# State space stage: decay factors of four of eight steps in three SBUF tiles, products with B up to four steps ahead, preparation dealt out by a table

## The chip, the cores and the metric

The kernel runs on one core of a Trainium2 chip. The core has engines that run side by side, each with its own queue of instructions in a fixed order: PE (TensorE, matrix products and transposes), DVE (VectorE), ACT (ScalarE), POOL (GpSimd) and SP (SyncE, which here issues all DMA transfers). Data lie in SBUF, a memory of 128 partitions that all engines reach, and in PSUM, eight small banks per partition, into which PE writes and which DVE and ACT can read and write. POOL works on SBUF alone in this kernel.

The metric is the time of one execution on the device in microseconds (us). Before the change it is 4334.76 us, the median of three runs (4333.15 to 4337.2). The profiled execution is one more run, with its own time.

## The reference

The model is a chain of six residual blocks over an input of 16 sequences (batches) of 512 positions with 256 channels, all float32: a feed-forward block with fp4 quantisation, a state space block (the block of this change), the feed-forward block again, a mixture of low-rank experts, attention with a distance bias, and the experts again. The state space block, cut to its core:

```python
xz = hidden_states @ W_in                      # 256 -> 2 * 512
x, z = jnp.split(xz, 2, axis=-1)
x = silu(causal_depthwise_conv(x, conv_w, 4 taps) + conv_b)
proj = x @ W_x                                 # dt_low (16), B (16), C (16)
dt = softplus(dt_low @ W_dt + b_dt)
A = -exp(A_log)                                # 512 channels x 16 states
def step(h, (dt_t, x_t, B_t, C_t)):
    h = exp(dt_t[..., None] * A) * h + (dt_t * x_t)[..., None] * B_t[:, None, :]
    return h, einsum('bds,bs->bd', h, C_t)
y = (scan over the 512 positions) + x * D
return (y * silu(z)) @ W_out
```

For each channel and each of 16 states this is a linear recurrence over 512 positions: h = a * h + b, with a the *decay factor* exp(dt * A) and b the *product with B*, dt * x * B. The result is multiplied with C and summed over the states.

## The kernel before

**Tiling.** `mamba_phase` (L469) walks through 16 batches `b`. A batch has four groups `c` of 128 channels and, in each group, eight *steps* `k`, so 32 steps per batch (`s`) and 512 in all (`t`). A step handles 128 channels and two of the 16 states per channel group: partitions hold four state groups of 32 channels each, and the free dimension holds two rows of 512 positions, 1024 elements. `k // 2` is the quarter `q` of the states, `k % 2` the half of the channels.

**One step.** ACT writes the decay factors with two activations (`factors`, L940: exp with a per-partition scale). POOL writes the product with B (`make_bx`, L863, tile `bx`). DVE runs the recurrence as one `tensor_tensor_scan` of 1024 elements (L971), whose inputs are the factors and the product. Column 0 of each row of the factors is zero, so that the second row starts afresh. The result is multiplied with C into a tile `g`: on DVE (L486) when the scan wrote to PSUM (tile `h`), on POOL (L483) when it wrote to SBUF (tile `hs`, two buffers); the flag `other` tells which. Before the change, POOL takes the product with C in steps 0, 2, 3 and, in even groups, 6. PE adds up the states: `accumulate` (L900) multiplies a pair of `g` tiles with a folding matrix into one PSUM bank `y`. After a group's last pair, `finish_mult` (L809) multiplies `y` into `zs` on DVE, right after the scan of step 0 of the next group.

**Where the inputs of the scan lie.** Two PSUM tiles `das` (two banks each) hold decay factors of the even and odd steps. In steps 4 and 5 (`turned`, quarter `TQ` = 2) it is the other way round: PE writes the product with B into the `das` tile with 32 small matmuls (`turn_bx`, L886; its second operand `diag` is made on POOL by `diagonals`, L874), and ACT writes the factors into one of two SBUF tiles `sides` (named `ds0` and `ds1`; the tile that holds dt, loaded from DRAM, is named `ds` too). So each of the eight scans has one input in PSUM and one in SBUF. After a turned scan DVE clears column 0 of its `das` tile again (L977).

**Order.** The order on every engine is the order in which the program issues (`keep_in_program_order`). In step `t` it issues: the product with B for step t + 2, the factors for step t + 1, the scan, `accumulate` for a pair that is due, the DMA issues of the step, one or two pieces of the preparation, `turn_bx` for step t + 2, and the product with C.

**Preparation.** `prepare` (L624) is a generator that computes all inputs of the next batch (transposes, input projection, the four convolution taps as four matmuls per channel group, W_x, softplus, dt * x, and the output projection of an earlier batch through `out_half`). Between its pieces it yields; 36 pieces per batch are dealt out, one per step, and two in steps 24, 26, 28 and 30. Most pieces are PE work that goes through a single PSUM bank (`mm`), followed by an ACT copy.

**Transfers.** SP issues all DMAs: `fetch_steps` (L553) loads dt and dt * x of the next channel group, spread over partitions, in two times four transfers, dealt out by the table `PIECES`; `fetch` (L541) loads a row pair of B and C, broadcast over partitions (tile `bc`); `later` writes dt and dt * x to DRAM.

Of the kernel before, what the change touches and what calls it, by code (L numbers as in the profile page):

```python
# [9 lines left out]
F32 = mybir.dt.float32  # L10
# [6 lines left out]
P = 128  # L17
NB, SEQ, D = 16, 512, 256
# [19 lines left out]
def macaron_kernel(  # L38
# [430 lines left out]
    def mamba_phase(w, src, dst):  # L469
        with tc.tile_pool(name="m1", bufs=1) as m1, tc.tile_pool(  # L470
# [17 lines left out]
            def pe(out, **kw):  # L488
                tc.keep_in_program_order(nc.tensor.matmul(out, **kw))  # L489
# [17 lines left out]
                nc.vector.memset(da[:, :, 0:1], 0.0)  # L507
                das.append(da)
            sides = []
            for i in range(2):  # L510
                da = m1.tile([P, 2, SEQ], F32, name=f"ds{i}")
                nc.gpsimd.memset(da[:, :, 0:1], 0.0)  # L512
                sides.append(da)
# [110 lines left out]
            def prepare(b):  # L624
# [15 lines left out]
                def taps(c):  # L640

                    if b == 0:
                        return
                    q = mm()
                    for k in range(DCONV):
                        pe(
                            q, lhsT=cwd[:, DCONV * c + k, :], rhs=xps[c % 2][:, k : k + SEQ],
                            start=(k == 0), stop=(k == DCONV - 1),
                        )
                    return q  # L650
# [47 lines left out]
                    to_xp(c, p)  # L698
                yield from project_out(0)
                for c in range(2):  # L700
                    p = taps(c)
                    yield
                    to_u(c, p)
                    p = in_proj(xT, c + 2)
                    yield
                    to_xp(c + 2, p)
                yield from project_out(1)
                for c in range(2, NDC):
                    p = taps(c)
                    yield  # L710
                    to_u(c, p)
                p = mm()
# [96 lines left out]
            def finish_mult(b, c, y):  # L809
                zs = zss[b]  # L810
                vec(zs[:, c, :], zs[:, c, :], y, ALU.mult)
# [27 lines left out]
            def close():  # L839

                for half in range(2):
                    for _ in range(6):
                        yield
                    for _ in out_half(NB - 2, half):
                        yield

            def where(t):
                return t // STEPS, t // NP % NDC, t % NP

            PIECES = (  # L850
# [4 lines left out]
            )  # L855
            bxs, ys, done = {}, [], []

            def run_later():
# [40 lines left out]

            def accumulate(b, c, q, gs):  # L900
                if q == 0:
                    ys.append(ps_y.tile([P, SEQ], F32, name="y", tag="y"))
                    u = state[b][0][c // 2][:, c % 2, :]
                    for i in range(0, P, 32):
                        pe(
                            ys[0][i : i + 32, :], lhsT=dskd[i : i + 32, c, :],
                            rhs=u[i : i + 32, :], start=True, stop=False,
                        )
                for i in range(4):
                    pe(  # L910
                        ys[0][32 * i : 32 * i + 32, :], lhsT=fold,
                        rhs=gs[i // 2][:, i % 2, :], start=False, stop=(q == NQ - 1),
                    )
                if q == NQ - 1:
                    done.append((b, c, ys.pop()))

            def flat(t):
                return t.rearrange("p n s -> p (n s)")
# [12 lines left out]
            for q in range(NQ):  # L931
                fetch(0, q)
            spare.clear()
            for t in range(2):
                make_bx(t)
            for _ in diagonals(0):
                pass
            for _ in range(4):
                next(rest)
            def factors(t):  # L940

                b, c, k = where(t)
                if b < NB:
                    q, p = k // 2, k % 2
                    da = (sides if q == TQ else das)[t % 2]
                    for j in range(2):
                        g = 4 * c + 2 * p + j
                        act(
                            da[:, j, 1:], spread[b, c, p][:, j, 0, 1:],
                            AF.Exp, scale=a_neg[:, g, q : q + 1],  # L950
                        )
# [3 lines left out]
            for t in range(STEPS * NB):  # L955
                b, c, k = where(t)
                s = t % STEPS
                if s == 0:
                    ahead = prepare(b + 1) if b + 1 < NB else close()
                    stat = stats(b + 2) if b + 2 <= NB else iter(())  # L960
                make_bx(t + 2)
                factors(t + 1)

                other = k in (0, 2, 3) or k == 6 and c % 2 == 0
                if other:
                    h = m2.tile([P, 2, SEQ], F32, name="hs", tag="hs", bufs=2)
                else:
                    h = ps_h.tile([P, 2, SEQ], F32, name="h", tag="h")
                turned = k // 2 == TQ
                da, bx = (sides, das) if turned else (das, bxs)  # L970
                tc.keep_in_program_order(nc.vector.tensor_tensor_scan(  # L971
                    flat(h), flat(da[t % 2]), flat(bx[t % 2] if turned else bx.pop(t)),
                    0.0, op0=ALU.mult, op1=ALU.add,
                ))
                if turned:
                    tc.keep_in_program_order(
                        nc.vector.memset(das[t % 2][:, :, 0:1], 0.0)  # L977
                    )

                if t in due:  # L980
                    accumulate(*due.pop(t))
                if s == 2:
                    load_out(b - 1)
                if s == 17:
                    load(b + 2)
                if 20 <= s < 24:
                    next(stat, None)

                if k == (0, 0, 0, 2)[c]:
                    steps = fetch_steps(*divmod(b * NDC + c + 1, NDC))  # L990
                for _ in range(PIECES[c][k]):
                    next(steps, None)
                run_later()
                if b and s == 0:
                    fetch(b, NQ - 1)
                if c == NDC - 1 and k in (2, 4, 6):
                    fetch(b + 1, k // 2 - 1)
                for _ in range(2 if t < 8 or s in (24, 26, 28, 30) else 1):
                    next(rest if t < 4 else ahead, None)
                turn_bx(t + 2)  # L1000
                g = m2.tile([P, 2, SEQ], F32, name="g", tag="g", bufs=5)
                C = rows[b, k // 2][:, 1:, :].to_broadcast([P, 2, SEQ])
                if other:
                    pool(g, h, C, ALU.mult)
                else:
                    vec(g, h, C, ALU.mult)
                if s == STEPS - 2:
                    diags = diagonals(b + 1)
                if t >= STEPS - 2 and s in (STEPS - 2, STEPS - 1, 0, 1):
                    next(diags, None)  # L1010
                pair.append(g)
                if k % 2:
                    due[t + 1 + other] = (b, c, k // 2, pair)
                    pair = []
                if k == 0 and done:
                    finish_mult(*done.pop())
                if s == STEPS - 1:
                    for _ in ahead:
                        pass
# [831 lines left out]
```

## Time and profile before

| what | value |
|---|---|
| median of three runs | 4334.76 us |
| time of the profiled execution | 4331.12 us |
| its span, first to last instruction | 4329.4 us |
| first scan of the stage starts at | 626.8 us |
| last scan of the stage starts at | 2503.6 us |
| 610 to 2506 us: PE busy | 1526.4 us of 1896 (80.5%), granted clock 0.90 |
| 610 to 2506 us: DVE busy | 1564.7 us (82.5%) |
| 610 to 2506 us: POOL busy | 1567.7 us (82.7%) |
| 610 to 2506 us: ACT busy | 1276.5 us (67.3%) |

The profiled execution took 1.7 us more than its span, and it lies 3.6 us under the median. Busy time is the time in which an engine has at least one instruction in work; the idle time that a row names is that of the engine just before the row's instructions, with the work that ended it. "Issue" stands where the engine waited for nothing that the profile shows. All the work of this change lies in the stage between about 610 and 2506 us; the other blocks are not touched.

### The profile page before, as it was taken

How to read it: one execution, taken by the hardware profiler on the slowest of the kernel's cores; microseconds unless marked ns; L12 is line 12 of the kernel's file. 1: busy time of each engine (PE TensorE's matmuls, PEld its weight loads, DVE VectorE, ACT ScalarE, POOL GpSimd, SP SyncE). 2: the span in 40 equal slices, each digit the busy share in tenths (PEclk: the TensorE clock that was granted, in tenths of full speed). 3: DMA queues.
4: the chain of work that ended last, by engine and by line, in shares of the span. 5: the costliest groups of instructions: out<-in, count | busy, mean ns of one | idle time of the engine just before them, and what ended most of it. 6: DMA issues, size and time to landing. Idle time of an engine off the chain costs nothing.

```text
span 4329.4 us, 68272 instructions
## 1 busy us (share of the span) xinstructions
PE 3833.4 (89%) x26498; PEld 2127.4 (49%) x26498; DVE 3629.7 (84%) x5002; ACT 2310.5 (53%) x3543; POOL 1844.9 (43%) x1687
## 2 busy tenths in 40 slices
PE   7999967888888888887888689999999999999989
PEld 4666632333333333333333356666765555555547
DVE  9999848888888888888888889998877888888876
ACT  4444337666666676677666534443534444444444
POOL 1000028888888888888888800000301111111121
PEclk9999988998999999999999889999999999999999
DMA  4000035444455545545444420000000000000002
GB/s 141 15 15 20 15 93 123 118 117 110 109 133 126 131 110 133 132 114 128 121 117 110 104 108 1 1 1 1 13 20 18 15 19 18 21 16 19 19 13 69
DMA packets 120471, 292.63 MB, mean 68 GB/s; under 512 B 30721, under 2 KB 50754, under 8 KB 120146
## 3 DMA queue, kind: packets, MB, share of 16 engines
q1 hardware_dynamic: 120146, 288.26, 26.2%
q8 instruction: 208, 3.41, 0.3%
q14 instruction: 117, 0.96, 0.1%
HBM read 209.26 MB, written 62.13 MB: 63 GB/s over the span
## 4 chain that ended last, share of the span: by engine, by line
PE 64%; DVE 13%; POOL 9%; ACT 7%; issue 3%; DMA 3%; SPq 1%; DVEq 0%; ACTq 0%; POOLq 0%
PE s L1180 10%; PE p L489 8%; PE g L289 7%; PE u L289 7%; PE o L325 7%; PE p L1180 4%; PE y L489 4%; POOL bx L483 4%; PE o L489 3%; PE p L1183 3%; POOL g L483 3%; DVE h L971 3%; PE da L489 3%; PE o L1180 3%; DMA ds<-dd 2%
## 5 line engine op out<-in xcount | busy, mean ns | idle before, releaser
L483 POOL TENSOR_TENSOR bx<-ds,bc 128x1024 f32<-128x1024 f32 x384 | 900.8, 2364 | 106.4 <-DVE h L971 91.7
L483 POOL TENSOR_TENSOR g<-hs,bc 128x1024 f32<-128x1024 f32 x224 | 526.9, 2365 | 201.6 <-DVE hs L971 196.7
L480 ACT ACTIVATE da<-ds,a_neg 128x511 f32<-128x511 f32 x768 | 526.7, 688 | 147.5 <-DVE da L977 73.0
L1351 ACT ACTIVATE eT<-s 128x768 f32<-128x768 f32 (+1 forms) x384 | 338.7, 882 | 420.3 <-PE s L1180 420.3
L1357 POOL TENSOR_SCALAR_AFFINE_SELECT eT<-eT 128x256 f32<-128x256 f32 (+1 forms) x384 | 189.9, 495 | 863.4 <-ACT eT L1351 863.4
L971 DVE TENSOR_TENSOR_SCAN hs<-da,bx 128x1024 f32<-128x1024 f32 x224 | 505.2, 2276 | 37.1 <-POOL bx L483 33.5
L489 PE MATMUL y<-g,fold 128*32 128x512 f32 x2048 | 380.0, 679 | 134.2 <-DVE g L486 101.7
L1180 PE MATMUL s<-k,q 32*128 32x256 f32 (+3 forms) x2048 | 459.6, 470 | 9.1 <-DVE mx L1311 5.8
L971 DVE TENSOR_TENSOR_SCAN h<-ds,da 128x1024 f32<-128x1024 f32 x128 | 293.8, 2296 | 171.9 <-issue 72.9
L971 DVE TENSOR_TENSOR_SCAN h<-da,bx 128x1024 f32<-128x1024 f32 x160 | 366.8, 2292 | 75.7 <-issue 27.4
L1311 DVE TENSOR_REDUCE mx<-s 128x2 f32<-128x1024 f32 (+3 forms) x512 | 410.1, 822 | 12.5
L1180 PE MATMUL s<-qm,k 32*128 32x512 f32 (+3 forms) x2048 | 385.7, 471 | 17.9 <-ACT eT L1351 11.4
L486 DVE TENSOR_TENSOR g<-h,bc 128x1024 f32<-128x1024 f32 x288 | 350.7, 1218 | 13.0
L1307 DVE TENSOR_TENSOR s<-s,mask 128x256 f32<-128x256 f32 (+1 forms) x384 | 198.8, 518 | 154.6 <-PE s L1180 144.4
L489 PE MATMUL p<-xT,w_in 128*128 128x512 f32 x500 | 271.6, 670 | 57.4 <-ACT dT L480 33.4
L294 ACT ACTIVATE sl<-g 128x352 f32<-128x352 f32 x256 | 118.3, 464 | 381.4 <-PE g L289 370.4
L1180 PEld LDWEIGHTS s<-k,q 32*128 32x128 f32 x2048 | 206.3, 185 | 171.1 <-issue 93.6
L1508 POOL TENSOR_TENSOR g<-rs,v 128x4 f32<-128x4 f32 x64 | 13.2, 211 | 635.7 <-ACT rs L1505 551.3
L489 PEld LDWEIGHTS da<-diag,dT 128*32 128x32 f32 x8192 | 220.8, 111 | 69.7 <-issue 42.0
L489 PE MATMUL da<-diag,dT 128*32 128x128 f32 x8192 | 250.4, 277 | 4.1 <-DVE hs L971 3.1
L489 PEld LDWEIGHTS y<-g,fold 128*32 128x32 f32 x2048 | 55.9, 113 | 368.3 <-DVE g L486 181.4
L512 POOL MEMSET ds<- 128x2 f32 x2 | 0.1, 102 | 531.5 <-DMA xd<-x 531.5
(286 smaller groups left out, 7957.7 us busy)
## 6 DMA issues: line engine op xcount, KB each, us to landing
ds<-dd SPq DMA_DIRECT2D x512, 256.0 KB, 5.2
bc<-bd SPq DMA_DIRECT2D x256, 128.0 KB, 5.6
dd<-dt SPq DMA_DIRECT2D x32, 1024.0 KB, 5.1
x<-_attn_hidden_states_dram SPq DMA_DIRECT2D x16, 512.0 KB, 6.6
xd<-x SPq DMA_DIRECT2D x16, 512.0 KB, 2.6
xo<-xd SPq DMA_DIRECT2D x16, 512.0 KB, 3.6
xe<-xo SPq DMA_DIRECT2D x16, 512.0 KB, 2.8
x<-xe SPq DMA_DIRECT2D x16, 512.0 KB, 10.7
```

What stands on the lines that cost most here:

```text
L289: nc.tensor.matmul(dst, lhsT=xT[:, k, c * P : (c + 1) * P], rhs=w[:, k, f0 : f0 + HF], start=(k == 0), stop=(k == KD - 1),)
L325: last = nc.tensor.matmul(o, lhsT=hT[:, f, :], rhs=wdT[:, f, :], start=(f == 0), stop=False)
L480: return tc.keep_in_program_order(nc.scalar.activation(out, in_, func, **kw))
L483: tc.keep_in_program_order(nc.gpsimd.tensor_tensor(out, in0, in1, op=op))
L486: tc.keep_in_program_order(nc.vector.tensor_tensor(out, in0, in1, op=op))
L489: tc.keep_in_program_order(nc.tensor.matmul(out, **kw))
L971: tc.keep_in_program_order(nc.vector.tensor_tensor_scan(flat(h), flat(da[t % 2]), flat(bx[t % 2] if turned else bx.pop(t)), 0.0, op0=ALU.m ...
L1180: tc.keep_in_program_order(nc.tensor.matmul(out, **kw))
L1307: nc.vector.tensor_tensor(own, own, const["mask"][:, :w].unsqueeze(1).to_broadcast([P, 2, w]), op=ALU.add)
L1311: nc.vector.tensor_reduce(mx[:, t, 2 * pair : 2 * pair + 2, RM], s[:, :, off : off + (t + 1) * P], axis=AX.X, op=ALU.max,)
L1351: const["exp"] = nc.scalar.activation(eT[:, 2 * pair : 2 * pair + 2, e0 : e0 + w], s[:, :, :w], AF.Exp)
L1357: nc.gpsimd.affine_select(out=own, in_=own, compare_op=ALU.is_ge, fill=0.0, base=0, pattern=[[0, 2], [0, n], [1, P]] if n > 1 else [[0, 2] ...
```

## The change

- A third SBUF tile for decay factors. The factors of steps 2, 3, 4 and 5 go to the three `sides` tiles in turn (`factors_at`); the `das` tiles hold the factors of steps 0, 1, 6 and 7 and the turned products of steps 4 and 5. The scans of steps 2 and 3 thereby read both inputs from SBUF.
- The table `FACTORS` says in which step factors are issued, and for how many steps ahead: one step ahead for steps 6, 7, 0 and 1, and two steps ahead for steps 2 to 5, behind the preparation of the issuing step.
- The table `PRODUCTS` does the same for the product with B: three or four steps ahead, behind the product with C of the issuing step. `bx` keeps three buffers.
- `turn_bx` for step 4 is issued in step 2, that for step 5 in step 4, in both cases ahead of the step's preparation.
- POOL takes the product with C in steps 0, 1, 3 and, in even groups, 5. `g` has four buffers where it had five.
- The table `PREPARED` says how many pieces of the preparation are done by each step of the batch (40, since `taps` now yields after two of its four matmul groups), at most three in a step.
- `diagonals` for the next batch is issued in steps 29 (two pieces), 30 and 31, where it was 30, 31, 0 and 1. `PIECES` gives group 1 its last four transfers in steps 1 and 2, where it had steps 3 and 4. `finish_mult` is issued ahead of the product with C of step 0, which is on POOL.

```diff
-            for i in range(2):
+            for i in range(3):
                 da = m1.tile([P, 2, SEQ], F32, name=f"ds{i}")
...
                     for k in range(DCONV):
+                        if k == 2:
+                            yield
                         pe(
...
-            PIECES = (
-                (4, 4, 0, 0, 0, 0, 0, 0),
-                (4, 0, 0, 2, 2, 0, 0, 0),
-                (4, 2, 2, 0, 0, 0, 0, 0),
-                (0, 0, 4, 4, 0, 0, 0, 0),
-            )
+            PIECES = ((4, 4, 0, 0), (4, 2, 2, 0), (4, 2, 2, 0), (0, 0, 4, 4))
+            PREPARED = (
+                (2, 4, 4, 4, 4, 5, 7, 8), (9, 11, 11, 12, 12, 13, 14, 15),
+                (16, 18, 18, 19, 21, 23, 25, 27), (30, 32, 33, 34, 35, 37, 39, 40),
+            )
+            FACTORS = ((1, 2), (2,), (2,), (2,), (), (1,), (1,), (1,))
+            PRODUCTS = ((3,), (), (4,), (4,), (4,), (), (3,), (3,))
...
-            for t in range(2):
+            for t in range(3):
                 make_bx(t)
...
+            def factors_at(t):
+                n, k = divmod(t, NP)
+                return sides[(4 * n + k - 2) % 3] if 2 <= k <= 5 else das[k % 2]
+
             def factors(t):
...
-                    da = (sides if q == TQ else das)[t % 2]
+                    da = factors_at(t)
...
-                make_bx(t + 2)
-                factors(t + 1)
-
-                other = k in (0, 2, 3) or k == 6 and c % 2 == 0
+                if k not in (1, 2, 3):
+                    for n in FACTORS[k][:1]:
+                        factors(t + n)
+
+                other = k in (0, 1, 3) or k == 5 and c % 2 == 0
...
-                da, bx = (sides, das) if turned else (das, bxs)
                 tc.keep_in_program_order(nc.vector.tensor_tensor_scan(
-                    flat(h), flat(da[t % 2]), flat(bx[t % 2] if turned else bx.pop(t)),
+                    flat(h), flat(factors_at(t)), flat(das[k % 2] if turned else bxs.pop(t)),
                     0.0, op0=ALU.mult, op1=ALU.add,
                 ))
...
                 if t in due:
                     accumulate(*due.pop(t))
+                if k == 2:
+                    turn_bx(t + 2)
+                if k == 4:
+                    turn_bx(t + 1)
...
-                for _ in range(2 if t < 8 or s in (24, 26, 28, 30) else 1):
-                    next(rest if t < 4 else ahead, None)
-                turn_bx(t + 2)
-                g = m2.tile([P, 2, SEQ], F32, name="g", tag="g", bufs=5)
+                if t < 4:
+                    for _ in range(2):
+                        next(rest, None)
+                else:
+                    for _ in range(min(3, PREPARED[c][k] - prepared)):
+                        next(ahead, None)
+                        prepared += 1
+                for n in FACTORS[k][k in (0, 4, 5, 6, 7):]:
+                    factors(t + n)
+                g = m2.tile([P, 2, SEQ], F32, name="g", tag="g", bufs=4)
                 C = rows[b, k // 2][:, 1:, :].to_broadcast([P, 2, SEQ])
+                if k == 0 and done:
+                    finish_mult(*done.pop())
                 if other:
                     pool(g, h, C, ALU.mult)
                 else:
                     vec(g, h, C, ALU.mult)
-                if s == STEPS - 2:
+                for n in PRODUCTS[k]:
+                    make_bx(t + n)
+                if s == STEPS - 3:
                     diags = diagonals(b + 1)
-                if t >= STEPS - 2 and s in (STEPS - 2, STEPS - 1, 0, 1):
+                    next(diags, None)
+                if s >= STEPS - 3:
                     next(diags, None)
...
-                if k == 0 and done:
-                    finish_mult(*done.pop())
```

More of the change, by code (lines that the diff above doesn't have):

```diff
@@ L700, in prepare @@
                 for c in range(2):
-                    p = taps(c)
+                    p = yield from taps(c)
                     yield
@@ L708, in prepare @@
                 for c in range(2, NDC):
-                    p = taps(c)
+                    p = yield from taps(c)
                     yield
@@ L958, in mamba_phase @@
                 if s == 0:
+                    prepared = 0
                     ahead = prepare(b + 1) if b + 1 < NB else close()
                     stat = stats(b + 2) if b + 2 <= NB else iter(())
-                make_bx(t + 2)
-                factors(t + 1)
-                other = k in (0, 2, 3) or k == 6 and c % 2 == 0
+                if k not in (1, 2, 3):
+                    for n in FACTORS[k][:1]:
+                        factors(t + n)
+                other = k in (0, 1, 3) or k == 5 and c % 2 == 0
                 if other:
@@ L976, in mamba_phase @@
                     tc.keep_in_program_order(
-                        nc.vector.memset(das[t % 2][:, :, 0:1], 0.0)
+                        nc.vector.memset(das[k % 2][:, :, 0:1], 0.0)
                     )
@@ L990, in mamba_phase @@
                     steps = fetch_steps(*divmod(b * NDC + c + 1, NDC))
-                for _ in range(PIECES[c][k]):
+                for _ in range(PIECES[c][k] if k < 4 else 0):
                     next(steps, None)
```

## The prediction

> **What bounds the kernel now.** First the busy time per stretch (columns PE, PEld, DVE, ACT, POOL, then the granted clock); 610 to 2506 us is the state space stage: PE, DVE and POOL all stand near 82%, none is full. Then the page's groups: POOL's long operations, and what ended the idle time before the scans.
>
> ```profile
> 610.00:2506.00 1896.00, 1526.37 (x12998) 670.41 (x12996) 1564.73 (x1111) 1276.54 (x1799) 1567.70 (x912) 0.90 0.50 120
> ...
> L483 POOL TENSOR_TENSOR bx<-ds,bc 128x1024 f32<-128x1024 f32 x384 | 900.8, 2364 | 106.4 <-DVE h L971 91.7
> L483 POOL TENSOR_TENSOR g<-hs,bc 128x1024 f32<-128x1024 f32 x224 | 526.9, 2365 | 201.6 <-DVE hs L971 196.7
> ...
> L971 DVE TENSOR_TENSOR_SCAN hs<-da,bx 128x1024 f32<-128x1024 f32 x224 | 505.2, 2276 | 37.1 <-POOL bx L483 33.5
> ...
> L971 DVE TENSOR_TENSOR_SCAN h<-ds,da 128x1024 f32<-128x1024 f32 x128 | 293.8, 2296 | 171.9 <-issue 72.9
> L971 DVE TENSOR_TENSOR_SCAN h<-da,bx 128x1024 f32<-128x1024 f32 x160 | 366.8, 2292 | 75.7 <-issue 27.4
> ```
>
> DVE's largest idle time stands before the turned scans (`h<-ds,da`, steps 4 and 5): 171.9 us. The timeline shows one such wait, step 4 of group 1:
>
> ```profile
> 1612.48 4.46 DVE L971 TENSOR_TENSOR_SCAN hs<-da,bx 128x1024 f32<-128x1024 f32 x2
> ...
> 1617.16 1.89 PE L489 MATMUL o<-w_out,zs 128*128 128x256 f32 x8
> ...
> 1618.98 1.96 PE L489 MATMUL da<-diag,dT 128*32 128x128 f32 x64
> ...
> 1621.06 2.30 DVE L971 TENSOR_TENSOR_SCAN h<-ds,da 128x1024 f32<-128x1024 f32 x1 [4.12 <-issue]
> ```
>
> Scans 2 and 3 end at 1616.9; PE does its preparation (`o`) first and turns afterwards, so scan 4 stands for 4.12 us. Last, what DVE and POOL do to each other, at the kernel's start, where POOL makes constants beside DVE operations that read two operands from SBUF:
>
> ```profile
> 30.87 1.62 DVE L166 SCALAR_TENSOR_TENSOR v<-c,v 128x1408 f32<-128x1408 f32 x1
> 32.42 1.21 DVE L168 TENSOR_TENSOR xq<-v,ns 128x1024 f32<-128x1024 f32 x1
> ...
> 31.08 2.70 POOL L451 TENSOR_SCALAR dskd<-fold,dsk 128x32 f32<-128x32 f32 x1
> ...
> 36.43 0.37 POOL L455 TENSOR_SCALAR cwd<-ident,ct 128x128 f32<-128x128 f32 x1
> ...
> 36.63 1.64 DVE L168 TENSOR_TENSOR q<-v,ns 128x1408 f32<-128x1408 f32 x1
> ...
> 36.78 1.77 POOL L455 TENSOR_SCALAR cwd<-ident,ct 128x128 f32<-128x128 f32 x1
> ```
>
> The `cwd` operation, 0.37 us, takes 1.77 when it begins during such a DVE operation, and ends 0.28 after it; `dskd` is held through two of them in a row. At 36.80 the first `cwd` ends, the next is queued, and DVE, 0.17 us into its operation, goes first. In the state space stage every DVE operation reads at most one tensor from SBUF, and there all 512 scans last 2.26 to 2.30 us beside a POOL that is 83% busy. So two SBUF inputs, not mere overlap, make the engines exclude each other. The scans of steps 2 and 3 become such operations.
>
> **The change, part by part.** The stage lasts from 626.8 to 2505.9 us (last scan's start plus its 2.3): 117.4 us for each of 16 batches.
>
> *Earlier turn and factors (gain).* `turn_bx` for step 4 goes ahead of PE's preparation and needs only scan 0 behind it; that for step 5 stands behind step 3's piece, at most half the taps (3.70/2 = 1.85 us). Factors of steps 2 to 5 run two steps ahead. At most this removes 171.9 us and the 75.7, 247.6 us or 15.5 a batch. I take it that DVE loses the 171.9; what is late next is POOL.
>
> *Two scans per group with two SBUF inputs (loss).* No row shows such a scan. Lower end: it excludes nothing, like today's 512 scans, and costs 0 (alone, two SBUF inputs don't slow DVE: L160's median on 1024 elements is 1218 ns, L486 takes 1224 with one). Upper end: it holds POOL off for its whole 2.28 us and waits up to 2.36 for a running POOL operation. A gain has no mechanism. I take the upper end, since the rows just shown are the nearest. That is 128 x 2.28 = 292 us on POOL's account: 1567.7 + 292 = 1860 us, 98.0 + 18.2 = 116.2 of 117.4 per batch. POOL may idle 1.2 us per batch for the time to stay; today it idles 19.4.
>
> The Trainium skill, "SBUF — State Buffer", section "Who interferes with whom", has a rule that speaks against this change: a Vector instruction with two SBUF inputs contends with a GpSimd instruction that reads SBUF, the one that issues first keeps the shared port for its whole length, and issue order decides who blocks. The rows agree on the blocking, but at 36.80 DVE went ahead of a POOL operation that followed its predecessor at once. By issue order alone, POOL's queue would pass each scan, and the sum would come out near 4490 us; by the rows it comes out as below. No run so far shows either for a scan.
>
> *Timetable by hand*: POOL operation 2.34 (two take 4.68), scan 2.20 (two take 4.46), scan with DVE's product 3.47 (1548.71 to 1552.17 for the like pair), `zs` 0.58; time 0 is the end of scan 3; a waiting scan goes first when POOL's operation ends.
> Even group: DVE does scans 4 to 7 and 0 by 14.8, `zs`, scan 1 by 17.6. POOL does bx6, g3, bx7, bx0, g5, bx1, bx2, g0 by 18.7. Scan 2 then holds the port to 20.9, bx3 to 23.3, scan 3 to 25.5; g1 is left over: 9 x 2.34 + 2 x 2.20.
> Odd group: no g5 on POOL, 1.2 us more on DVE. POOL does the old g1, bx6, g3, bx7, bx0, bx1, bx2, g0, by 18.7; scan 1 ends at 18.9, so bx3 goes first, to 21.1; scan 2 to 23.3, g1 to 25.6, scan 3 to 27.8. No idle time either.
> Four groups: 2 x 53.3 = 106.6. POOL's other work per batch: dt * x 4 x 1.27 = 5.1, the normalisation's small operations 3.0 (1565.43 to 1568.43), `diag` 4 x 0.64 = 2.5: 10.6. Sum 117.2. A handover saves some 0.1 (the held `cwd` ended 0.28 after DVE, not 0.37): 16 x 0.1 = 1.6 less, 115.6.
>
> *Waits that the table leaves out.* Scans wait for 84.6 us elsewhere today (75.7, and 37.1 less the first scan's 28.1), `finish_mult` 42.4 for PE's `y`: 127 us, 7.9 a batch. POOL has 1.1 (even) or 2.2 us (odd) to work off while scan 2 waits, so part is covered; I count half, 4.0, and keep 0 and 7.9 as ends.
>
> *Edits costed at nothing.* 256 more activations write SBUF: 711 instead of 691 ns, 5 us in all, under ACT's 33% of idle; without that, 5 us. Four `g` tiles: g4 needs the first pair's accumulation, 1.1 to 2 us on PE after g1; g1 comes 2.3 after scan 3 in odd groups, g4 3.4 after: nothing spare, up to 1 us late, within POOL's lead there. The taps' extra pauses issue nothing. `diag` moves ahead of POOL's step 0, its 2.5 us stay. Group 1's moved transfers (SP, 1.74 us per four issues) land in 5.2, a step or more before use. bx0 of the next batch is asked for in step 28 instead of 30: its `ds` and `bc`, issued in step 26, land 5.2 to 5.6 us later, and in the table POOL reaches bx0 some 14 us after scan 2. In step 26 SP stands behind the write of dt * x, which waits for POOL's second pair (2.5 us); `bc` behind it still has 6. If that cover went, each us late costs 16. The third tile's memset, 0.1 us, falls into 531.5 us of POOL's idle time.
>
> Sum: 115.6 + 4.0 = 119.6, 2.2 a batch more, +35 us on the profiled execution's 4331.1: 4366; with its 3.6 under the median, **4370 us**. Ends 115.6 and 123.5 give 4306 and 4432, the likeliest case's own range.
>
> **The rivals.**
> *The old waits of steps 4 and 5 stay (slower; the change then doesn't do what it says).* PE or ACT could be late at the new places too: 10.7 us per batch, less POOL's lead of 2 x 1.1 + 2 x 2.2 = 6.6: 4.1 more, about 4435; with 1 us per group beyond that, 4500. For it: PE is 80% busy and runs in order. Against: the 1.96 us turn has no piece in front in step 4's case. It decides from 2 us late per group.
> *POOL keeps the port (slower).* If POOL's next ready operation always passes a waiting scan, scan 2 waits for g0, bx3, g1 and bx6: 29.9 us in an even group, 31.1 in an odd one, and about 5 of the other 10.6 show: 127, +9.6 x 16, 4490. For it: POOL's operations follow without a gap. Against: at 36.80 DVE went first.
> *The port is free, or held in part (faster).* A scan takes 2.2 ns per element where L486 takes 1.2; it may leave POOL room. Then DVE sets the pace: 23.3 us in even and 24.6 in odd groups, 95.8 per batch, 2.4 for the statistics, 2.6 for `zs`, some 6 of POOL's other work: 107; PE, busy 95.4 us per batch, would be at 89%, so up to 113. That is 4168 to 4264, 4216 at 110. It decides the sign once a scan holds POOL for less than 2.28 - 2.2/8 = 2.0 us.
>
> **How the numbers follow.** Likeliest case 62%; old waits stay 16%; POOL keeps the port 7%; port free or partly held 15%. A difference of 0.2% (8.7 us) is about what a measurement of this kernel can tell. The likeliest case lies around 4370 with a width of some 60: 17 of its 62 below 4326, 6 within, 39 above. Faster 17 + 15 = 32%, same 6%, slower 39 + 23 = 62%. The range leaves out the lower half of the last case and the far end of the slow ones: 4215 to 4490.
>
> **What the profile would show.** Right: a new form of scan that reads `ds` and `bx`, 64 times into `h` and 64 times into `hs`, many over 2.3 us, or POOL's `bx` and `g` beside them up to 4.6; POOL's busy time in the stage at 1750 us or more; turned scans nearly without idle time. Wrong: those scans at 2.28 and POOL at 2.36 (third rival); turned scans still idle (first); scans beside several POOL operations in a row (second). What would upset it all is a late transfer that I took as covered.

## The result, and the profile after

The changed kernel takes 4398.2 us (median of four runs, 4394.1 to 4402.2) against 4334.6 us: ratio 1.0146, 95% interval 1.0128 to 1.0164. It is 64 us slower. The forecast was 4370, slower with a chance of 62%, and 4306 to 4432 for the likeliest case.

The profiled execution has a span of 4392.4 us, 63.0 more than before. All of it lies in the state space stage, whose scans now run from 629.5 to 2569.5 us (626.8 to 2505.9 before). By the starts of the scans in the two traces, batches 1 to 14 take 121.1 us each instead of 117.9 (44 us together), the first batch takes 11 us more, the last 6, and the first scan starts 3 later.

First the stage as one window of the changed kernel: its length, then the busy time and instructions of PE, PEld (PE's weight loads), DVE, ACT and POOL, then the granted clock (the share of PE's full clock that the profile records, 1 being full), DMA share and GB/s:

```profile
610.00:2570.00 1960.00, 1530.40 (x13003) 688.60 (x13001) 1727.61 (x1111) 1271.53 (x1801) 1791.39 (x912) 0.93 0.48 116
```

POOL's two groups on the page:

```profile
L483 POOL TENSOR_TENSOR bx<-ds,bc 128x1024 f32<-128x1024 f32 x384 | 1002.1, 2617 | 61.0 <-DVE h L979 45.1
L483 POOL TENSOR_TENSOR g<-hs,bc 128x1024 f32<-128x1024 f32 x224 | 620.5, 2770 | 78.3 <-DVE hs L979 68.5
```

And the scans within the window, by form:

```profile
L979 DVE TENSOR_TENSOR_SCAN h<-da,bx 128x1024 f32<-128x1024 f32 x128 | 293.9, 2296 | 15.6 <-ACT da L480 2.0 <-POOL bx L483 0.8 <-DVE g L486 0.5
L979 DVE TENSOR_TENSOR_SCAN hs<-da,bx 128x1024 f32<-128x1024 f32 x128 | 292.3, 2284 | 85.4 <-ACT da L480 49.5 <-POOL bx L483 35.7
L979 DVE TENSOR_TENSOR_SCAN h<-ds,bx 128x1024 f32<-128x1024 f32 x64 | 229.7, 3589 | 58.2 <-ACT ds L480 58.2
L979 DVE TENSOR_TENSOR_SCAN hs<-ds,bx 128x1024 f32<-128x1024 f32 x64 | 223.7, 3495 | 31.8 <-ACT ds L480 26.4 <-POOL bx L483 5.4
L979 DVE TENSOR_TENSOR_SCAN h<-ds,da 128x1024 f32<-128x1024 f32 x96 | 218.6, 2277 | 24.6 <-PE da L489 16.3 <-ACT ds L480 5.1
L979 DVE TENSOR_TENSOR_SCAN hs<-ds,da 128x1024 f32<-128x1024 f32 x32 | 72.9, 2279 | 2.3 <-ACT ds L480 2.3
```

Two things are to be read here. The idle time before the turned scans (`ds,da`) is nearly gone: 24.6 + 2.3 = 27 us instead of 172. And the new form `ds,bx`, with two SBUF inputs, takes 3.5 to 3.6 us instead of 2.28, while POOL's products grew from 2.36 to 2.62 and 2.77. DVE's account closes: busy 1727.6 - 1564.7 = 163 us more, idle (1960 - 1727.6) - (1896 - 1564.7) = 232 - 331 = 99 less, together 64.

One such pair in the timeline of the changed kernel, DVE and POOL:

```profile
1554.86 2.35 POOL L483 TENSOR_TENSOR bx<-ds,bc 128x1024 f32<-128x1024 f32 x1
...
1555.10 4.27 DVE L979 TENSOR_TENSOR_SCAN h<-ds,bx 128x1024 f32<-128x1024 f32 x1
...
1557.18 4.35 POOL L483 TENSOR_TENSOR g<-hs,bc 128x1024 f32<-128x1024 f32 x1
...
1560.55 3.13 DVE L979 TENSOR_TENSOR_SCAN hs<-ds,bx 128x1024 f32<-128x1024 f32 x1
...
1561.49 4.34 POOL L483 TENSOR_TENSOR bx<-ds,bc 128x1024 f32<-128x1024 f32 x1
```

Scan 2 is issued at 1555.10, 0.24 us after POOL's `bx`. It ends 2.16 us after that `bx` ends at 1557.21, which is a whole scan. POOL's next operation, queued without a gap, is passed by the scan, ends at 1561.53, and so takes 2.16 us from the scan's end at 1559.37. Scan 3 waits again for it. So a scan holds POOL off for its length, as the rows from the kernel's start showed for shorter operations. Here, and for most of the scans, a waiting scan goes ahead of POOL's next operation, but not always. In batches 0 to 14 of the changed kernel the scan of step 2 in group 3 is passed by one short operation (dt * x; at 1587.22, 0.02 us after the scan at 1587.20 shown below). In `noload_after`, a variant described below, two of the 128 scans are passed by five operations in a row, until POOL has nothing more to do:

```profile
974.75 11.95 DVE L979 TENSOR_TENSOR_SCAN h<-ds,bx 128x1024 f32<-128x1024 f32 x1 [0.78 <-issue]
975.06 2.37 POOL L483 TENSOR_TENSOR bx<-ds,bc 128x1024 f32<-128x1024 f32 x1
...
977.37 2.52 POOL L483 TENSOR_TENSOR dt<-dt,u 128x512 f32<-128x512 f32 x2
...
979.85 2.37 POOL L483 TENSOR_TENSOR g<-hs,bc 128x1024 f32<-128x1024 f32 x1
...
982.16 2.38 POOL L483 TENSOR_TENSOR bx<-ds,bc 128x1024 f32<-128x1024 f32 x1
```

That scan is issued 0.37 us before POOL's running operation ends. Others in the same run, issued as shortly before such an end, went first and took 2.52 us, so what decides between the two is open.

The third thing is new: scans 1, 2 and 3 now wait for ACT (`<-ACT ds`, `<-ACT da`). One case in step 2 of group 3:

```profile
1581.69 1.28 ACT L480 ACT_TABLE_LOAD   x1
1582.99 1.06 ACT L480 ACTIVATE dt<-dt 128x1024 f32<-128x1024 f32 x1
1584.06 1.28 ACT L598 ACT_TABLE_LOAD   x1
...
1585.80 1.32 ACT L480 ACTIVATE ds<-ds,a_neg 128x511 f32<-128x511 f32 x2
...
1587.20 3.45 DVE L979 TENSOR_TENSOR_SCAN h<-ds,bx 128x1024 f32<-128x1024 f32 x1 [3.73 <-ACT ds L480]
```

The factors (`ds<-ds,a_neg`) are issued behind the pieces of their step; here softplus stands in front with two loads of ACT's function tables (1.28 us each), and DVE waits 3.73 us.

### The profile page after: what moved, and what is told of

The parts are those of the page before. It is cut to its first block, busy times and chain, and to the rows that moved or that the text cites. A ratio compares the mean times of both kernels' runs of the same rounds, so it can differ in the third digit from the quotient of the medians.

```text
span 4392.4 us, 68394 instructions
## 1 busy us (share of the span) xinstructions
PE 3838.7 (87%) x26498; PEld 2146.3 (49%) x26498; DVE 3791.1 (86%) x5002; ACT 2307.5 (53%) x3546; POOL 2067.6 (47%) x1688
## 4 chain that ended last, share of the span: by engine, by line
PE 60%; ACT 13%; DVE 12%; DMA 6%; POOL 5%; issue 5%; SPq 1%; DVEq 0%; ACTq 0%; POOLq 0%
PE s L1201 10%; PE p L489 8%; PE g L289 7%; PE u L289 7%; PE o L325 7%; PE p L1201 4%; DVE h L979 4%; PE p L1204 3%; ACT da L480 3%; ACT L480 3%; PE o L1201 3%; DMA ds<-dd 3%; DMA bc<-bd 2%; PE y L489 2%; PE da L489 2%
## 5 line engine op out<-in xcount | busy, mean ns | idle before, releaser
L483 POOL TENSOR_TENSOR bx<-ds,bc 128x1024 f32<-128x1024 f32 x384 | 1002.1, 2617 | 61.0 <-DVE h L979 45.1
L483 POOL TENSOR_TENSOR g<-hs,bc 128x1024 f32<-128x1024 f32 x224 | 620.5, 2770 | 78.3 <-DVE hs L979 68.5
L480 ACT ACTIVATE da<-ds,a_neg 128x511 f32<-128x511 f32 x512 | 353.1, 690 | 273.3 <-DVE da L985 219.9
L489 PE MATMUL y<-g,fold 128*32 128x512 f32 x2048 | 354.6, 613 | 106.7 <-POOL g L483 64.5
L489 PE MATMUL p<-xT,w_in 128*128 128x512 f32 x500 | 314.5, 761 | 69.5 <-ACT dT L480 31.4
L979 DVE TENSOR_TENSOR_SCAN hs<-da,bx 128x1024 f32<-128x1024 f32 x128 | 292.3, 2284 | 85.4 <-ACT da L480 49.5
L480 ACT ACTIVATE ds<-ds,a_neg 128x511 f32<-128x511 f32 x512 | 332.1, 710 | 19.6 <-DVE h L979 19.4
L979 DVE TENSOR_TENSOR_SCAN h<-da,bx 128x1024 f32<-128x1024 f32 x128 | 293.9, 2296 | 15.6 <-ACT da L480 2.0
L489 PE MATMUL p<-xp,cwd 128*128 128x512 f32 x480 | 231.0, 613 | 58.7 <-ACT xo L480 36.1
L979 DVE TENSOR_TENSOR_SCAN h<-ds,bx 128x1024 f32<-128x1024 f32 x64 | 229.7, 3589 | 58.2 <-ACT ds L480 58.2
```

What stands on the lines that cost most here:

```text
L480: return tc.keep_in_program_order(nc.scalar.activation(out, in_, func, **kw))
L483: tc.keep_in_program_order(nc.gpsimd.tensor_tensor(out, in0, in1, op=op))
L979: tc.keep_in_program_order(nc.vector.tensor_tensor_scan(flat(h), flat(factors_at(t)), flat(das[k % 2] if turned else bxs.pop(t)), 0.0, op0 ...
```

## The experiments

Theory A: the exclusion between POOL and the scans of steps 2 and 3 is the loss. Rival B: the loss is ACT's factors behind the preparation. Later rivals grew out of the results. A ratio is that to the kernel before in the same session, with its 95% interval.

**Does the loss go when no scan has two SBUF inputs?** Two variants of the changed kernel, `port_in1` and `port_in0`, let scans 2 and 3 read a PSUM tile in place of one SBUF input:

```diff
-                    flat(h), flat(factors_at(t)), flat(das[k % 2] if turned else bxs.pop(t)),
+                    flat(h), flat(factors_at(t)),
+                    flat(das[k % 2] if turned or k in (2, 3) else bxs.pop(t)),
```
```diff
-                    flat(h), flat(factors_at(t)), flat(das[k % 2] if turned else bxs.pop(t)),
+                    flat(h), flat(das[k % 2] if k in (2, 3) else factors_at(t)),
+                    flat(das[k % 2] if turned else bxs.pop(t)),
```

> The changed kernel, but the scans of steps 2 and 3 read their second input from the PSUM tile da in place of bx; all of POOL's products are still made, and the state of these two steps is left wrong. Theory A (the two-input scans and POOL exclude each other): the stretch of these scans, by the trace some 10.3 us per batch on DVE and 220 us in all on POOL's operations, goes away, all 512 scans last 2.26 to 2.30 us, POOL's products 2.36, and the time falls by 130 to 200 us to 4200 to 4270. Theory B (the loss is ACT's factors coming late behind the preparation, 5.6 us per batch before scans 2 and 3, and the port costs nothing on the path): these waits stay, the time stays at 4380 to 4400.

> The changed kernel, but the scans of steps 2 and 3 read their first input from the PSUM tile da in place of the SBUF factors, which are still made; the state of these two steps is left wrong. It takes away both the exclusion and the wait for ACT's factors of steps 2 and 3, but keeps the wait for bx. Theory A: 4150 to 4250, below the other variant by up to 90 us (5.6 us x 16). Theory B: 4300 to 4320, all of it from the 90 us of waits for ACT.

Measured: 4361.0 us (ratio 1.0063, 1.0048 to 1.0078) and 4360.4 us (1.0064, 1.0049 to 1.0079). All 512 scans last 2.3 us or less and POOL's products 2.36, yet only some 37 of the 64 us come back. Neither theory's figure holds.

**Was that gain cut short?** In these variants scan 2 reads `da0`, so PE's turn for step 4 waits for scan 2 and the preparation is queued behind it. `port_free` reads `da1` in both scans:

```diff
-                    flat(h), flat(factors_at(t)), flat(das[k % 2] if turned else bxs.pop(t)),
+                    flat(h), flat(factors_at(t)),
+                    flat(das[1] if k in (2, 3) else das[k % 2] if turned else bxs.pop(t)),
```

> The changed kernel with scans 2 and 3 both reading their second input from the PSUM tile da1 in place of bx (state left wrong). In the two earlier variants the tile da0 was read by scan 2 as well, so that PE's turn for step 4 had to wait for scan 2, with the preparation queued behind it; here it waits for scan 0 only, as in the changed kernel. Theory A (the exclusion of scans and POOL is the loss; the 37 us measured so far were cut short by that added wait): 4240 to 4335, at least 60 us under the changed kernel. Theory G (behind the port stand PE and ACT: turns behind pieces, factors behind function tables): 4345 to 4375, as before.

Measured: 4361.1 us (1.0059, 1.0046 to 1.0073). The added wait had cost nothing; theory G's figure. Its stage as a window:

```profile
610.00:2535.00 1925.00, 1527.21 (x13004) 683.67 (x13002) 1573.50 (x1111) 1268.73 (x1801) 1569.42 (x912) 0.91 0.49 119
```

Three of its groups of scans, by form (steps 2 and 3 now count under `ds,da`):

```profile
L979 DVE TENSOR_TENSOR_SCAN h<-ds,da 128x1024 f32<-128x1024 f32 x160 | 365.2, 2282 | 130.8 <-PE da L489 84.2 <-ACT ds L480 46.5
...
L979 DVE TENSOR_TENSOR_SCAN hs<-da,bx 128x1024 f32<-128x1024 f32 x128 | 292.3, 2283 | 87.7 <-ACT da L480 54.6 <-POOL bx L483 33.1
L979 DVE TENSOR_TENSOR_SCAN hs<-ds,da 128x1024 f32<-128x1024 f32 x96 | 219.1, 2282 | 60.1 <-ACT ds L480 34.0 <-PE da L489 22.4 <-ACT da L480 1.7
```

DVE's busy time falls by 154 us against the changed kernel (1573.5), but its idle time rises from 232 to 351 us. The waits for PE's turned product, 16.3 us in the changed kernel, are back at 84 + 22 = 107 us. So the stretched scans had covered most of them. The likely way, not tested by itself: with a scan that takes 1.2 us longer, PE has that much more time to turn.

**One part undone.** `psum23` puts the factors of steps 2 and 3 back into PSUM, early in their step, and keeps the rest:

```diff
-                return sides[(4 * n + k - 2) % 3] if 2 <= k <= 5 else das[k % 2]
+                return sides[(2 * n + k - 4) % 3] if 4 <= k <= 5 else das[k % 2]
...
-            FACTORS = ((1, 2), (2,), (2,), (2,), (), (1,), (1,), (1,))
+            FACTORS = ((1,), (1,), (1, 2), (2,), (), (1,), (1,), (1,))
...
-                if k not in (1, 2, 3):
+                if k != 3:
...
-                for n in FACTORS[k][k in (0, 4, 5, 6, 7):]:
+                for n in FACTORS[k][k != 3:]:
```

> The changed kernel with one part undone: the factors of steps 2 and 3 go to the PSUM tiles again, one step ahead and ahead of the preparation; the earlier turn, the tables for products and preparation and the moved diagonals stay. Theory A: no scan has two SBUF inputs, the 4 and 5 waits stay gone: 4210 to 4290, faster than the kernel before. Theory B: the factors of steps 2 and 3 depend on the scan two steps back again and the other moves bring nothing: 4330 to 4400.

Measured: 4376.6 us (1.0099, 1.0084 to 1.0114). This is inside theory B's range and far from A's: a complete kernel without any two-input scan, and it is slower than before. In it the turn for step 4 waits for scan 2 again, as in `port_in1`.

**One part alone.** `before_sides` is the kernel before with the factors of steps 2 to 5 in three SBUF tiles:

```diff
-            for i in range(2):
+            for i in range(3):
                 da = m1.tile([P, 2, SEQ], F32, name=f"ds{i}")
...
-                    da = (sides if q == TQ else das)[t % 2]
+                    da = factors_at(t)
...
-                g = m2.tile([P, 2, SEQ], F32, name="g", tag="g", bufs=5)
+                g = m2.tile([P, 2, SEQ], F32, name="g", tag="g", bufs=4)
```

> The kernel before with one part of the change alone: factors of steps 2 to 5 in three SBUF tiles (and four g tiles for room), in the old order. Theory A: the exclusion comes without the earlier turn's gain: 4400 to 4500. Theory B: the only effect is that the turn no longer waits for scans 2 and 3: 4270 to 4335.

Measured: 4397.6 us (1.0147, 1.0130 to 1.0164), at the edge of theory A's range and far from B's. In the old order the SBUF factors, with four `g` tiles instead of five, cost 65 us. So far there are four corners: old order without two-input scans 4333 and with them 4398; new order without them 4361 and with them 4398. In the new order only one input of the scans was changed, the first or the second with the same result, so there the exclusion costs 37 us. The 65 us of the old order are a net figure: the lost `g` tile is in it, and so is a gain, since DVE's wait before the turned scans falls from 172 to 97 us there. The new order costs 28 us or nothing.

**The earlier turn alone.** `before_turn` moves `turn_bx` in the kernel before, nothing else. No scan has two SBUF inputs. The move goes further than that of the change: the turn stands ahead of `accumulate` too, and that for step 5 already in step 3.

```diff
+                turn_bx(t + 2)
                 if t in due:
                     accumulate(*due.pop(t))
...
                     next(rest if t < 4 else ahead, None)
-                turn_bx(t + 2)
```

> The kernel before with one change: turn_bx goes ahead of accumulate and of the preparation's piece in its step. No scan has two SBUF inputs. Theory E: the 4.1 us before step 4 in group 1 and part of the 3.1 us in group 3 go, 3 to 6 us per batch: 4240 to 4290. Theory F: the pieces that come later make something else wait, 4325 to 4345.

Measured: 4517.3 us (1.0426, 1.0409 to 1.0444), 184 us slower and against both theories. The groups of this kernel, with what ended the idle time before them:

```profile
L489 PE MATMUL da<-diag,dT 128*32 128x128 f32 x8192 | 312.4, 317 | 136.8 <-DVE hs L971 135.2
L971 DVE TENSOR_TENSOR_SCAN h<-ds,da 128x1024 f32<-128x1024 f32 x128 | 293.8, 2296 | 248.3 <-ACT ds L480 131.2 <-PE da L489 70.7 <-issue 44.3
L489 PEld LDWEIGHTS da<-diag,dT 128*32 128x32 f32 x8192 | 266.6, 129 | 210.6 <-DVE hs L971 168.8 <-issue 21.7 <-DVE st L582 10.6
```

The weight loads of the same group in the kernel before, and then in the changed kernel:

```profile
L489 PEld LDWEIGHTS da<-diag,dT 128*32 128x32 f32 x8192 | 220.8, 111 | 69.7 <-issue 42.0 <-DVE hs L971 27.3
```
```profile
L489 PEld LDWEIGHTS da<-diag,dT 128*32 128x32 f32 x8192 | 236.8, 115 | 113.2 <-issue 60.4 <-DVE hs L979 29.2 <-DVE g L486 19.5
```

PE stands in front of the turn until the scan that reads the tile ends (168.8 us before weight loads, 27.3 in the kernel before), and accumulation and preparation are queued behind. The piece in front of the turn had filled that time. DVE's wait before the turned scans grows from 172 to 248 us. In the changed kernel PE waits there for 29.2 us only: with the factors of steps 2 and 3 in SBUF, the PSUM tile is free after scans 0 and 1. How much of the 184 us comes from the place ahead of `accumulate` was not measured. `psum23`, whose early turns stand behind `accumulate` and whose turn for step 5 comes in step 4, has its factors in PSUM as well and is 44 us slower than before, not 184.

`turn_port` tries the last late turn, that of step 5, on `port_in1`:

```diff
+                if k == 3:
+                    turn_bx(t + 2)
                 if t in due:
                     accumulate(*due.pop(t))
                 if k == 2:
                     turn_bx(t + 2)
-                if k == 4:
-                    turn_bx(t + 1)
```

> The changed kernel with scans 2 and 3 reading their second input from PSUM in place of bx (state left wrong; 4361 us so far), and the turn for step 5 issued in step 3, ahead of accumulate and of the piece, where it was step 4. Theory E (without the port's stretch, PE's turned products, above all that of step 5 behind step 3's piece, set the pace): the waits before step 5 in groups 1 and 2, 2.0 and 1.6 us, and part of the 0.7 in group 3 go: 4290 to 4325. Theory F (the pace is PE's whole chain, so that the place of one turn changes nothing): 4350 to 4375.

Measured: 4386.4 us (1.0124, 1.0108 to 1.0139), outside both theories' ranges and 25 us slower than with the turn in step 4, although the wait before step 5 is gone. It comes back before DVE's own products with C, which wait 97 us for PE's accumulation (`y`), where `port_in1` has 1.9:

```profile
L486 DVE TENSOR_TENSOR g<-h,bc 128x1024 f32<-128x1024 f32 x288 | 351.8, 1222 | 109.9 <-PE y L489 97.0 <-DVE h L979 0.5 <-issue 0.3
```

The accumulation, queued behind the turn, is what frees a `g` tile.

**ACT's table loads.** `noload_after`, the changed kernel:

```diff
-                            act(us[0], us[0], AF.Silu)
+                            act(us[0], us[0], AF.Exp, scale=0.01)
...
-                    act(dt[:, :, 0, :], dt[:, :, 0, :], AF.Softplus)
+                    act(dt[:, :, 0, :], dt[:, :, 0, :], AF.Exp, scale=0.01)
...
```

> The changed kernel with Silu and Softplus of the stage replaced by exp of 0.01 x, so that ACT loads no function tables between them and the decay factors (170 loads of 1.28 us fewer; the values are wrong). Theory B (ACT's factors come late behind the table loads, 8.9 us per batch before scans 1, 2 and 3): 4250 to 4320. Theory A' (POOL and the port pace): 4350 to 4400, the waits move to POOL.

Measured: 4373.5 us (1.0093, 1.0078 to 1.0108). ACT's busy time falls by 225 us to 1046.8 and the waits before scans 1 and 2 shrink, but only 25 us come back, within theory A' and not B. The scans stay stretched (3.77 and 3.37 us in the mean of steps 2 and 3, with two of nearly 12 us).

**PE's share.** Three kernels compute one of the four convolution taps: `light_before`, `light_after` and `light_port` (on `port_in1`). The edit of `light_after`; `light_before` does the same to the kernel before:

```diff
                     for k in range(DCONV):
                         if k == 2:
                             yield
-                        pe(
-                            q, lhsT=cwd[:, DCONV * c + k, :], rhs=xps[c % 2][:, k : k + SEQ],
-                            start=(k == 0), stop=(k == DCONV - 1),
-                        )
+                        if k == 0:
+                            pe(
+                                q, lhsT=cwd[:, DCONV * c + k, :], rhs=xps[c % 2][:, k : k + SEQ],
+                                start=True, stop=True,
+                            )
```

> The kernel before with one of the four convolution taps on PE (three matmul pairs per channel group and batch left out, some 10 us of PE's work per batch; the convolution is not complete). Theory C (PE's fixed order paces the stage as soon as DVE and POOL are not held up): the waits of step 4 shrink and the time falls by 60 to 140 us to 4190 to 4275. Theory D (PE has room, 80% busy; the rest is chance of the order): less than 30 us.

> The changed kernel with one of the four taps on PE. Theory A' (the exclusion of scans and POOL paces this kernel, not PE): POOL stays at 92% and the time falls by less than 50 us, to 4350 to 4395. Theory C (PE paces it): 4250 to 4330.

> The changed kernel with one of the four taps on PE and with the scans of steps 2 and 3 reading their second input from PSUM in place of bx (state left wrong). Theory C: both held resources are eased, the waits for PE's turned product go and the time falls by 80 to 160 us from 4361, to 4200 to 4280. Theory D: it stays above 4330. If the loss from the port is hidden behind PE, the difference to the changed kernel with one tap is larger here than the 38 us measured with four taps.

Measured: `light_before` 4254.4 us (0.9820, 0.9804 to 0.9836), 78 less, theory C. `light_after` 4464.5 us (1.0305, 1.0290 to 1.0320), 66 *more* than with four taps, and `light_port` 4385.9 us (1.0125, 1.0110 to 1.0140), 25 more: theory D's figure for this one (above 4330), but no theory had less work make a kernel slower. Between the last two, which differ in the scans' second input alone, lie 79 us, where four taps gave 37. With less work on PE the exclusion costs more, as the expectation of `light_port` said for a loss that is in part hidden behind PE. The stages of `light_before` and `light_after`:

```profile
610.00:2432.00 1822.00, 1412.44 (x12639) 606.56 (x12637) 1563.42 (x1111) 1280.27 (x1799) 1568.23 (x912) 0.88 0.52 125
```
```profile
610.00:2636.00 2026.00, 1496.72 (x12636) 653.64 (x12636) 1739.41 (x1111) 1264.39 (x1797) 1792.98 (x912) 0.86 0.48 113
```

The taps left out are three quarters of the convolution's group, 231 us in the changed kernel, so 173 us. PE's busy time falls by 114 us in the one and by only 34 in the other, whose granted clock is 0.86 instead of 0.93. A lower clock is a candidate for the 66 us: in the changed order the missing work may leave PE idle long enough for its clock to be halved more often, and the input projection's matmuls take 824 ns instead of 763 in the mean. The sizes fit: by the windows, the shortfall from the full clock grows from 0.07 x 1960 = 137 us to 0.14 x 2026 = 284 in the changed order, and only from 0.10 x 1896 = 190 to 0.12 x 1822 = 219 in the old one. Against it as the whole cause: `light_before` loses some clock as well and is still faster, and the changed kernel takes 763 ns at 0.93 where the kernel before takes 669 at 0.90, so where these matmuls stand counts too. No run held the clock fixed; the cause stays open.

**A try for a faster kernel.** `best` is `before_turn` with the SBUF factors of steps 4 and 5 issued two steps ahead and the last Silu moved to step 4 of the next batch:

```diff
-                factors(t + 1)
+                if k not in (3, 4):
+                    factors(t + 1)
+                if k in (2, 3):
+                    factors(t + 2)
...
+                if s == 4:
+                    for _ in last:
+                        pass
                 if s == STEPS - 1:
-                    for _ in ahead:
-                        pass
+                    last = ahead
```

> The kernel before with the earlier turn, the SBUF factors of steps 4 and 5 two steps ahead (two tiles as before), and the last Silu of the preparation in step 4 of the next batch, where it stood in front of the factors of step 1. Theory E: besides the turn's 3 to 6 us per batch, the 2.3 us before step 4 and 2.7 us before step 1 in group 0 go: 4160 to 4240. Theory F: 4290 to 4340, PE being no freer.

Measured: 4459.4 us (1.0292, 1.0276 to 1.0307), far above both theories' ranges. The two additions win 58 us over `before_turn`, and the earlier turn loses more. Nothing that computes the whole result beat the kernel before.

## Why the prediction was right or wrong

*Two scans per group with two SBUF inputs.* Right in mechanism, and for the form of scan that no row had shown. The term was too large: POOL's account grew by 1791.4 - 1567.7 = 224 us, 1.75 per scan, not 2.28 (292 us). Some scans run while POOL has nothing to do (the shortest lasts 2.27 us), and a held operation needs 2.16 us after the scan, not 2.36. On DVE, where the prediction priced nothing directly, the busy time grew by 163 us, nearly all of it in these scans.

*The timetable.* It let POOL work without idle time, 115.6 us a batch plus 4.0 of other waits. Measured in batches 1 to 14 are 121.1 us, of which POOL is busy for 111.8 and idle for 9.3. Two errors partly cancel: POOL has 3.8 us a batch less to do than the 115.6, and idles for 9.3 where 4.0 were allowed. The sum came out 28 us low, inside the likeliest case's range, and the closeness is in part luck. About half of the 28 us comes from these batches, which grew by 44 us where 2.2 each, 31 us, were forecast. The rest comes from the two ends of the stage, which grew by some 20 us where 4 were forecast.

*Earlier turn: "I take it that DVE loses the 171.9".* DVE did, down to 27 us, but not for the reason given. `port_free` shows that without the stretch 107 us of waits for the turned product stay. *"What is late next is POOL"* held only in part. The stretch of the scans, some 163 us, is a wait for POOL, and without it the kernel gains 37 us. But in DVE's idle time ACT's factors come next (92 us before scans that read `ds`, 51.5 before `da` in the changed kernel) and only then POOL's products (42 us, 31 of them before the first scan); and behind POOL stands PE, as `port_free` shows. The rival "the old waits stay" describes the waits of `port_free`, which is 28 us over the kernel before; in the changed kernel the stretched scans hide them.

*Edits costed at nothing.* ACT's 256 activations were priced by duration, 5 us in ACT's idle time. Their place was not priced: behind the step's pieces, with two table loads in front of them once per batch. This is a missing term. Its size is not settled: without any of the stage's Silu and Softplus loads, `noload_after` got 25 us back, while two of its scans lost over 9 us each to POOL. The first batch's 11 us were left out as well; their cause was not tested.

*Rivals.* "POOL keeps the port", as a rule for every scan, is refuted: the scan at 1555.10 passed POOL's queued product, and no scan of the changed kernel took more than 4.41 us. As an event it exists: the two scans of `noload_after` that took nearly 12 us, and three of `before_sides` that took 7.7 us behind three operations, waited just as this rival says. The prediction also took it that by issue order POOL would pass every scan. By the starts in the trace that does not follow: the scan (1555.10) began ahead of POOL's next product (1557.18) and went first, while the one at 974.75 began ahead of POOL's product (975.06) and lost. So the order of starts alone does not decide. "The port is free" is refuted by scans of up to 4.41 us. Its price was wrong too: with no exclusion the kernel takes 4361 us, not 4168 to 4264, and what DVE then waits for before its scans is mostly PE's turned products and ACT's factors.

*What stays open.* Without the exclusion the new order is 28 us slower than the old, nearly half of the loss of 64 us, and no run shows which part of it costs this. PE, ACT, DVE and POOL all idle there, and moving one wait moved another. Which entry of the preparation table is responsible was not tried.

## What to carry to other kernels

When four engines are each some 80% busy and run fixed orders, a wait that the trace names is often the shadow of another; price a removal by the next wait in the queue, and expect the gain to be a fraction of the idle time. Before a product moves ahead of filler work on an engine with a fixed order, ask what it waits for there: the filler may be what hides the wait, and a buffer that comes free earlier may have to come with it. Count the SBUF inputs of a DVE operation that runs beside POOL: in these runs the second one turned two engines into one for its length, and in a few cases POOL passed the waiting scan several times in a row.

## What the runs showed of the hardware that was not expected

Less work on PE made the changed kernel 66 us slower, with the stage's granted clock at 0.86 instead of 0.93. At the lower clock the same four matmuls of the input projection take 3.78 us instead of 1.98 (changed kernel, at 1619.24 and 1581.73; the granted clock over the two is 0.51 and 1.00). The Trainium skill, "TensorE: Matmul & The Clock Gate", section "Part 1: The HAM clock gate (the "warmup" mystery)", says that PE falls to half its clock after an idle window of about 3.4 us and recovers after a busy one; the two durations agree with the half, the window itself was not tested.

A scan that takes 2.2 ns per element, about twice an elementwise product, still keeps POOL out for its whole length: a product queued at 1557.18 behind the scan took 4.35 us. Which of the two engines goes first is not fixed: scans with 0.37 us to wait for POOL's running operation took 2.52 us or, in two cases, nearly 12.
